# Layer 0's positional products: two bands of four offset rows side by side, in place of one block of eight

## The chip, the cores and the metric

The kernel runs on one core of one Trainium2 chip. The metric is the device time of that core for one execution, in microseconds. Before the change its median over three runs is 1242.21 us (1241.89 to 1242.93).

A core has several engines that run side by side, each through its own list of instructions in a fixed order: TensorE (PE, matrix products; PEld is its loading of weights), VectorE (DVE), ScalarE (ACT), GpSimd (POOL) and SyncE (SP), which here only issues transfers (DMAs). They wait for one another by semaphores. PSUM is the memory that TensorE writes its products to, in banks of 128 partitions by 512 fp32 numbers; SBUF is the working memory.

## The reference, cut to what matters

The input is four images of 16 x 16 positions and 1024 channels. Layer 0 is a lambda layer: queries q for four heads, keys k and values v, and two terms, one by content and one by position:

```python
q = bn(einsum('bhwc,cd->bhwd', x, Wq)); k = x @ Wk; v = bn(x @ Wv)   # x is group-normalised
q = q.reshape(b, heads, 256, m); k = softmax(k.reshape(b, 1, 256, m)); v = v.reshape(b, 1, 256, m)
Lc  = einsum('bukm,buvm->bkv', k, v)
Yc  = einsum('bhkn,bkv->bnhv', q, Lc)
rel = rel_pos_emb[rel_pos[..., 0], rel_pos[..., 1]]   # rel_pos = pos[m] - pos[n] + 15, in both directions
Lp  = einsum('nmku,buvm->bnkv', rel, v)
Yp  = einsum('bhkn,bnkv->bnhv', q, Lp)
x   = x + Yc + Yp
```

Layer 1 is causal attention with 16 heads and then a mixture of eight experts, each behind a layer norm. The change touches only the positional term of layer 0.

A position n is a row ni and a column nj of the 16 x 16 grid, likewise m. The table rel_pos_emb has 31 x 31 offsets with 256 numbers each; position n needs the entry (mi - ni + 15, mj - nj + 15) for every m.

## The kernel before, in words

**The order of the sums.** The kernel never forms Lc or Lp. It first makes one matrix of scores, s0[m, n, bh] = sum over the 256 key channels of (k[m] + rel[n, m]) times q[n, bh], for the 16 pairs bh of image and head, and then multiplies s0 with v (the products `py`, line 559).

**The positional scores (lines 446 to 482).** For one column nj, the 16 offsets mj - nj + 15 are 16 neighbouring columns of the table, and a whole row of offsets can serve every ni. So the loop takes the offset rows in blocks R of eight, in the order 1, 2, 0, 3. For each R and each of the 16 nj, GpSimd copies a window of the table (`emb`, two halves of 128 channels, eight offset rows by 16 columns) into one of four buffers (line 462). TensorE takes the window as its weights, 128 x 128 for each channel half, and streams past it the queries of all ni that need any of these rows: 16, 15, 8 and 7 rows ni for R = 1, 2, 0, 3, times the 16 bh (line 464). The result has 128 partitions, one for each offset row and mj. ScalarE and VectorE in turn copy two or four nj at a time out of PSUM into `two_T` (line 472).

In `two_T` a partition means an offset row; in s0 it means a row mi, and which one depends on ni. That shift is made by transfers: for each ni, one or two DMAs on SyncE's queue (line 479) move the right partitions of `two_T` to their partitions of s0, which holds mi in two halves of eight rows. There are 60 of them. Blocks 0 and 3 reuse the half of `two_T` that block 1 was copied out of.

**What stands around it.** Before it come the q and k products (lines 376 and 407); the k products already use the two column halves of TensorE side by side, each with 64 columns of weights. After it come the v products (`v_product`, line 493), seven of them with four pieces each, which read the normalised input `xn`. Then `x_at`, the raw input in eight tiles of 128 tokens, is loaded on SyncE's queue (line 537). It lies in the same buffer as `xn`, so its first load waits for the last v product.

Then comes a loop over the eight tiles (lines 547 to 577), first the four with positions ni >= 8 and then the four with ni < 8. `content(b, nt)` (line 422) adds the content scores to that half of s0; the products `py` multiply s0 with v; VectorE adds them to `x_at` (line 566) and a layer norm follows. The banks for `pT`, `py` and half of `pc` come from a tag "mm" with three banks (line 123):

```python
    def mm(name):
        return ps.tile([P, HALF], F32, tag="mm", name=name)
```

**What sets the order.** Inside `tc.manual_schedule(engines={SP, DVE})`, which begins after x_at's loads, SyncE and VectorE keep the order in which the loop is written. Elsewhere a planner sets each engine's order when the kernel is built; it may take a later instruction first where an earlier one isn't ready. In the profile, some products of line 496 stand ahead of those of line 464. SyncE's queue is one list: the table's load (line 241), the load of w_kv, the 60 copies of line 479, the eight loads of x_at, the load of w_v, and the transfers of the layer norms.

Of the kernel before, what the change touches and what calls it, by code (L numbers as in the profile page):

```python
# [32 lines left out]
F32 = mybir.dt.float32  # L33
# [6 lines left out]
P = 128  # L40
# [7 lines left out]
BH = B * HEADS0  # L48
SIDE = 16
REL = 2 * SIDE - 1  # L50
GROUP = 32
H = 16
D = C // H
# [2 lines left out]
HALF = 512  # L56
# [11 lines left out]
def kernel(  # L68
# [27 lines left out]
    nc = tc.nc  # L96

    def pool(stack, name, bufs=1, **kw):
        return stack.enter_context(tc.tile_pool(name=name, bufs=bufs, reuse_waits="tile", **kw))
# [10 lines left out]
    def big_tile(n, name, shape=(NC, TOK)):  # L110
        return big[n].tile([P, *shape], F32, tag="big", name=name)
# [11 lines left out]
    def mm(name):  # L123
        return ps.tile([P, HALF], F32, tag="mm", name=name)
# [85 lines left out]
    with ExitStack() as layer0:  # L210
# [9 lines left out]
        for i, a in enumerate((v_gamma, v_beta, v_mean, v_var)):  # L220
            nc.gpsimd.dma_start(vp[:, i, :], a)
        emb = l0.tile([P, 2, REL, REL], F32, tag="emb", name="emb")
        v_T = l0.tile([P, 2, TOK], F32, tag="v_T", name="v_T")

        q0 = l0.tile([P, 2, SIDE, SIDE, BH], F32, tag="q0", name="q0")

        with ExitStack() as projection:
# [3 lines left out]
            nc.vector.memset(average, 0.0)  # L231
            for g in range(P // GROUP):
                nc.vector.memset(average[ts(g, GROUP), ts(g, GROUP)], 1.0 / GROUP)
            first_root = small.tile([P, 1], F32, tag="first_root", name="first_root", bufs=1)
# [3 lines left out]
            q_scale, q_shift, mean_q, var_q = (q_rows[:, i, :] for i in range(4))  # L238
            for t, a in ((var_q, q_var), (q_scale, q_gamma), (mean_q, q_mean), (q_shift, q_beta)):
                nc.sync.dma_start(t, a.partition_broadcast(P))  # L240
            nc.sync.dma_start(emb.rearrange("p c i j -> p c (i j)"), embT)


            chunks = {}
# [72 lines left out]
            with tc.manual_schedule():  # L317
# [6 lines left out]
                for c in range(NC):  # L324
# [10 lines left out]
                    elif NC - 4 < c < NC - 1:  # L335
                        n = c - (NC - 3)
# [12 lines left out]
            parts = big_tile(0, "q_parts").rearrange("p a b -> p (a b)")  # L349
            b11, b12, b21, b22 = (w_q[l][:, 4 * j : 4 * j + 4, :] for j in range(2) for l in range(2))  # L350
            pairs = []
            for pair in range(2):
                a = [xn[:, 4 * j : 4 * j + 4, ts(4 + 2 * pair + i, P)] for i in range(2) for j in range(2)]
                homes = [parts[:, ts(8 * pair + i, HALF)] for i in range(8)]
# [47 lines left out]
            for t in range(NT):  # L402
                b, kc = divmod(t, 2)
                pk = (tr if t % 2 else mm)(f"pk{t}")
                for c in range(NC):
                    for kl in range(2):
# [4 lines left out]
                            start=(c == 0),  # L411
                            stop=(c == NC - 1),
# [28 lines left out]
        S2 = SIDE // 2  # L441
        s0 = big_tile(0, "s0", (2, SIDE, SIDE, BH))
        tpool = pool(layer0, "tpool", 2)
        two_T = big_tile(1, "two_T", (2, SIDE, SIDE, BH))

        for R, first, n_i, T in (
            (1, 0, 16, two_T[:, 0, :, :, :]),
            (2, 0, 15, two_T[:, 1, :15, :, :]),
            (0, 8, 8, two_T[:, 0, :8, :, :]),
            (3, 0, 7, two_T[:, 0, 8:15, :, :]),  # L450
        ):
            rows = min(S2, REL - S2 * R)
            parts = rows * SIDE
            group = 2 if n_i > S2 else 4
            for n0 in range(0, SIDE, group):
                pT = mm(f"pT{R}_{n0}")
                out_T = pT[:parts, : group * BH * n_i].rearrange("p (j i h) -> p j i h", j=group, h=BH)
                for g in range(group):
                    nj = n0 + g
                    at = SIDE - 1 - nj  # L460
                    window = tpool.tile([P, 2, rows, SIDE], F32, tag="window", name=f"window{R}_{nj}", bufs=4, padded_shape=[P, 2, S2, SIDE])
                    nc.gpsimd.tensor_copy(window, emb[:, :, S2 * R : S2 * R + rows, at : at + SIDE])
                    for kc in range(2):
                        nc.tensor.matmul(  # L464
                            out_T[:, g, :, :],
                            window[:, kc, :, :].rearrange("p i j -> p (i j)"),
                            q0[:, kc, first : first + n_i, nj, :],
                            start=(kc == 0),
                            stop=(kc == 1),
                        )  # L470
                evict = nc.scalar.copy if n0 // group % 2 == 0 else nc.vector.tensor_copy
                evict(T[:parts, :, n0 : n0 + group, :].rearrange("p i j h -> p j i h"), out_T)
            for i in range(n_i):
                ni = first + i
                start = S2 * R + ni - SIDE + 1
                for mh in range(2):
                    lo, hi = max(start, mh * S2), min(start + rows, mh * S2 + S2)
                    if lo < hi:
                        nc.sync.dma_start(
                            s0[(lo - mh * S2) * SIDE : (hi - mh * S2) * SIDE, mh, ni, :, :],  # L480
                            T[(lo - start) * SIDE : (hi - start) * SIDE, i, :, :],
                        )

# [63 lines left out]
        with tc.manual_schedule(engines={mybir.EngineType.SP, mybir.EngineType.DVE}):  # L547
            for i, (b, nt) in enumerate(tiles):
# [5 lines left out]
                for hp in range(2):  # L554
                    py = mm(f"py{t}_{hp}")
                    for hl in range(2):
                        bh = b * HEADS0 + 2 * hp + hl
                        for mh in range(2):
# [4 lines left out]
                                start=(mh == 0),  # L563
                                stop=(mh == 1),
# [16 lines left out]
    with ExitStack() as attention:  # L581
# [18 lines left out]
        T = [s_pool.tile([P, NC // 2, HALF], F32, tag=f"T{i}", name=f"T{i}", bufs=1) for i in range(3)]  # L600
# [275 lines left out]
    rows = dram.tile([TOK, C], F32, name="rows")  # L876
# [83 lines left out]
    with ExitStack() as gating:  # L960
# [306 lines left out]
        w, bias, step, T, T3, A, S = {0: w0}, {0: bias0[0]}, {}, {}, {}, {}, {}  # L1267
# [243 lines left out]
def _laid_out(inputs):  # L1511
    import numpy as np

    def get(name):
        return np.asarray(inputs[name])

    def columns(a):
        return a.reshape(-1, P).T
# [3 lines left out]

    emb = get("L0_conv_rel_pos_emb").reshape(REL * REL, 64, 2, 2).transpose(3, 1, 2, 0)
    return {
# [42 lines left out]
```

## Time and profile before

| what | value |
| --- | --- |
| median of 3 runs | 1242.21 us |
| the profiled execution's own time | 1242.44 us |
| its span | 1240.6 us |
| granted TensorE clock, mean | 0.999 |
| TensorE busy | 1224.4 us |
| VectorE, ScalarE, GpSimd busy | 740.2, 221.1, 390.8 us |
| positional products, line 464 | 148.47 to 188.68 us |
| copies into s0, line 479 | issued from 163.31 to 203.9 us |
| x_at's loads, line 537 | issued from 210.35 us |

The span is the time from the first to the last instruction of the core in the profile. A line of a view names the line of the code, the engine, the operation, the tile written and those read, the shapes, and a count. In the list of groups, the figures behind the bar are the busy time in us, the mean length of one in ns, and the idle time of the engine ahead of them. In the view in order of time, the first two figures are start and length in us, and a square bracket says how long the engine had been idle and for what it waited. In the list of waits, the figures are us in all, how often, and the longest.

### The profile page before, as it was taken

How to read it: one execution, taken by the hardware profiler on the slowest of the kernel's cores; microseconds unless marked ns; L12 is line 12 of the kernel's file. 1: busy time of each engine (PE TensorE's matmuls, PEld its weight loads, DVE VectorE, ACT ScalarE, POOL GpSimd, SP SyncE). 2: the span in 40 equal slices, each digit the busy share in tenths (PEclk: the TensorE clock that was granted, in tenths of full speed). 3: DMA queues.
4: the chain of work that ended last, by engine and by line, in shares of the span. 5: the costliest groups of instructions: out<-in, count | busy, mean ns of one | idle time of the engine just before them, and what ended most of it. 6: DMA issues, size and time to landing. Idle time of an engine off the chain costs nothing.

```text
span 1240.6 us, 12777 instructions
## 1 busy us (share of the span) xinstructions
PE 1224.4 (99%) x4540; PEld 639.8 (52%) x4540; DVE 740.2 (60%) x1322; ACT 221.1 (18%) x515; POOL 390.8 (31%) x471
## 2 busy tenths in 40 slices
PE   9999999999999999999999999999999999999998
PEld 5445894778884444444444444444344434434443
DVE  5796626677333666657554867766656656565642
ACT  3310111130001222223121431101111111111110
POOL 1041360340000222222230115445452735363521
PEclk9999999999999999999999999999999999999999
DMA  9002024842201535353393557383855575556432
GB/s 350 21 1 84 2 75 127 308 153 85 68 17 52 157 104 168 102 176 105 108 278 111 207 202 250 71 238 85 242 135 166 110 229 155 150 138 187 101 82 54
DMA packets 91495, 169.22 MB, mean 136 GB/s; under 512 B 9344, under 2 KB 46224, under 8 KB 91424
## 3 DMA queue, kind: packets, MB, share of 16 engines
q1 hardware_dynamic: 74064, 115.83, 27.9%
q0 software_dynamic: 15136, 47.78, 16.1%
q10 hardware_dynamic: 2224, 4.72, 1.1%
q8 instruction: 38, 0.62, 0.2%
q14 instruction: 33, 0.27, 0.1%
HBM read 115.59 MB, written 48.50 MB: 132 GB/s over the span
## 4 chain that ended last, share of the span: by engine, by line
PE 74%; DVE 3%; ACT 1%; issue 0%; DVEq 0%; ACTq 0%
PE p L1334 31%; PE pqk L616 16%; PE po L798 7%; PE pv L616 7%; PE left L1376 3%; PE sc L711 2%; PE pa L780 2%; PE rest L1390 2%; PE last_pe L1492 1%; PE dense_pe L918 1%; PE parts L1056 0%; ACT L132 0%; DVE row_T L177 0%; DVE xb L800 0%; DVE T L1277 0%
## 5 line engine op out<-in xcount | busy, mean ns | idle before, releaser
L903 POOL DMA_INDIRECT w_e_xg<-rows,gather x146 | 158.0, 1082 | 57.3 <-issue 40.8
L1334 PE MATMUL p<-w_e,A 128*128 128x512 f32 x368 | 163.2, 593 | 1.3 <-DVE slot L1169 1.3
L753 POOL TENSOR_TENSOR s_q<-s_q,total 128x128 f32<-128x128 f32 (+1 forms) x128 | 66.2, 547 | 300.3 <-DVE total L750 297.9
L798 PE MATMUL po<-w_p,y_T 128*128 128x512 f32 x256 | 118.5, 605 | 0.0
L1334 PEld LDWEIGHTS p<-w_e,A 128*128 128x128 f32 x368 | 69.6, 190 | 89.9 <-issue 89.9
L1334 PE MATMUL p<-T,S 128*128 128x512 f32 x256 | 112.7, 592 | 0.0
L926 POOL DMA_INDIRECT out_dram<-y,add x32 | 56.6, 1770 | 176.0 <-ACT y L1340 112.5
L1340 ACT ACTIVATE y<-y,slot 128x512 f32<-128x512 f32 x64 | 46.0, 722 | 330.6 <-DVE y L1348 165.2
L739 ACT ACTIVATE s_q<-s,top 128x256 f32<-128x256 f32 (+1 forms) x128 | 56.6, 444 | 186.1 <-issue 142.0
L616 PE MATMUL pqk<-ln,w_qk 128*128 128x512 f32 x192 | 85.6, 595 | 0.0
L1334 PEld LDWEIGHTS p<-T,S 128*128 128x128 f32 x256 | 48.6, 190 | 60.8 <-issue 60.5
L798 PEld LDWEIGHTS po<-w_p,y_T 128*128 128x128 f32 x256 | 45.9, 190 | 47.9 <-issue 46.9
L177 DVE STREAM_TRANSPOSE A<-w_e_xg 128x1024 f32<-128x1024 f32 x32 | 39.6, 1238 | 50.1 <-DMA w_e_xg<-rows,gather 50.1
L616 PE MATMUL pqk<-T,S_qk 128*128 128x512 f32 x128 | 58.5, 599 | 0.0
L616 PEld LDWEIGHTS pqk<-ln,w_qk 128*128 128x128 f32 x192 | 36.0, 190 | 43.3 <-issue 42.3
L1334 PE MATMUL p<-w_e,S 128*128 128x512 f32 x128 | 57.5, 592 | 0.0
L1334 PE MATMUL p<-T,A 128*128 128x512 f32 x128 | 57.5, 592 | 0.0
L616 PE MATMUL pv<-w_v,ln 128*128 128x256 f32 x192 | 44.2, 381 | 1.4 <-DVE ln L177 0.9
L295 PE MATMUL pq<-w_q,xn 128*128 128x512 f32 x96 | 44.5, 599 | 0.3 <-ACT xn L275 0.3
L1376 PE MATMUL left<-w_e,one 128*32 128x512 f32 x312 | 41.8, 593 | 0.0
L464 PE MATMUL pT<-q,window 128*128 128x256 f32 (+3 forms) x256 | 40.4, 320 | 0.0
L1334 PEld LDWEIGHTS p<-w_e,S 128*128 128x128 f32 x128 | 24.3, 190 | 30.6 <-issue 30.4
(317 smaller groups left out, 1871.8 us busy)
## 6 DMA issues: line engine op xcount, KB each, us to landing
w_e<-in_expert_w_dram SPq DMA_DIRECT2D x14, 2048.0 KB, 15.1
s_rows<-s_q SPq DMA_DIRECT2D x32, 384.0 KB, 2.7
s_rows<-s_rows SPq DMA_DIRECT2D x128, 96.0 KB, 2.2
w_qk<-in_W_attnT_dram SPq DMA_DIRECT2D x8, 1024.0 KB, 6.1
xn<-in_xT_dram SPq DMA_DIRECT2D x8, 512.0 KB, 7.5
w_q<-in_Wq_dram SPq DMA_DIRECT2D x16, 256.0 KB, 7.3
x_at<-in_x_dram SPq DMA_DIRECT2D x8, 512.0 KB, 4.8
w_v<-in_W_attnT_dram SPq DMA_DIRECT2D x2, 2048.0 KB, 14.5
```

Of the source, the lines that this page charges most:

```text
L177: nc.vector.transpose(row_T[:, :, :slots].rearrange("p c (g j) -> p g c j", j=32), row[:, : slots // 32, :].rearrange("p g (c i) -> p g c ...
L295: nc.tensor.matmul(pq, xn[:, c, ts(t, P)], w_q[kc][:, c, :], start=(c == 0), stop=(c == NC - 1))
L464: nc.tensor.matmul(out_T[:, g, :, :], window[:, kc, :, :].rearrange("p i j -> p (i j)"), q0[:, kc, first : first + n_i, nj, :], start=(kc ...
L616: nc.tensor.matmul(bank, stationary(c), moving(c), start=(c == 0), stop=(c == NC // 2 - 1))
L739: nc.scalar.activation(blocks(h, qt), s[:, h, cols].rearrange("p (b f i) -> p b f i", f=Q, i=32), AF.Exp, bias=top[:, qt, h : h + 1], accu ...
L753: nc.gpsimd.tensor_mul(blocks(h, qt), blocks(h, qt), total[:, qt, h : h + 1].unsqueeze(2).unsqueeze(3).to_broadcast([P, 1 + qt, Q, 32]),)
L798: nc.tensor.matmul(po, y_T[:, c, ts(t, P)], w_p[j][:, c, :], start=(c == 0), stop=(c == NC - 1))
L903: nc.gpsimd.indirect_dma_start(out=row[:, g, :], out_offset=None, in_=table[: (TOK - P) * Q, :] if e in SHORT else table, in_offset=bass.I ...
L926: nc.gpsimd.indirect_dma_start(out=out[: TOK - P, :] if e in SHORT else out, out_offset=bass.IndirectOffsetOnAxis(ap=add[:slots, e, k : k ...
L1334: nc.tensor.matmul(bank, a[:, c, :], b[:, c, :], start=(c == 0), stop=(c == NC // 2 - 1))
L1340: nc.scalar.mul(y[i][:, ts(j, HALF)], y[i][:, ts(j, HALF)], slot[:, e, 1, 2 * pair + i : 2 * pair + i + 1])
L1376: nc.tensor.matmul(bank[ts(i, 32), :], stationary, w[of][j][:, c, :], start=(c == 0), stop=(c == NC - 1))
```

## The change

The offset rows are taken in bands of four instead of blocks of eight. Two bands, one from below the middle and one from above it, are taken together: (3, 4), (2, 5), (1, 6), (0, 7). Each gives 64 columns of weights (48 for band 7, which has three rows), and the two use the two column halves of TensorE, so that they can stream different rows ni at the same time: 16, 12, 8 and 4 rows for the four pairs. The table is loaded in band order, by eight DMAs in place of one, so that a pair's rows lie side by side and one copy makes the window for both. In the last two pairs VectorE makes every second window. There are six window buffers in place of four.

The copies into s0 are listed as they become possible and issued in another order: after the first pair those with ni < 8, which frees the place that the third pair's results need, then those with ni >= 8; after every other pair those with ni >= 8; and at the end all that are left. They still stand ahead of x_at's loads in the program.

```diff
+BAND = 4
+BANDS = ((3, 4), (2, 5), (1, 6), (0, 7))
...
-            nc.sync.dma_start(emb.rearrange("p c i j -> p c (i j)"), embT)
+            at = 0
+            for band in (b for both in BANDS for b in both):
+                rows = min(BAND, REL - BAND * band)
+                nc.sync.dma_start(
+                    emb[:, :, at : at + rows, :].rearrange("p c i j -> p c (i j)"),
+                    embT[:, :, BAND * REL * band : (BAND * band + rows) * REL],
+                )
+                at += rows
...
-        for R, first, n_i, T in (
-            (1, 0, 16, two_T[:, 0, :, :, :]),
-            (2, 0, 15, two_T[:, 1, :15, :, :]),
-            (0, 8, 8, two_T[:, 0, :8, :, :]),
-            (3, 0, 7, two_T[:, 0, 8:15, :, :]),
-        ):
-            rows = min(S2, REL - S2 * R)
-            parts = rows * SIDE
-            group = 2 if n_i > S2 else 4
+        moves = []
+
+        def bands(k, half, band, n, first, T):
+            rows = min(BAND, REL - BAND * band)
+            for i in range(n):
+                ni = first + i
+                start = SIDE - 1 - ni
+                for mh in range(2):
+                    lo = max(BAND * band - start, mh * S2)
+                    hi = min(BAND * band + rows - start, mh * S2 + S2)
+                    if lo < hi:
+                        at = half * 64 + (lo + start - BAND * band) * SIDE
+                        to = s0[(lo - mh * S2) * SIDE : (hi - mh * S2) * SIDE, mh, ni, :, :]
+                        moves.append((k, ni, to, T[at : at + (hi - lo) * SIDE, i, :, :]))
+
+        def move(which):
+            for m in [m for m in moves if which(*m[:2])]:
+                nc.sync.dma_start(*m[2:])
+                moves.remove(m)
+
+        homes = (two_T[:, 0, :, :, :], two_T[:, 1, :12, :, :], two_T[:, 0, :8, :, :], two_T[:, 1, 12:, :, :])
+        for k, ((low, high), T) in enumerate(zip(BANDS, homes)):
+            n_i = BAND * (low + 1)
+            firsts = SIDE - n_i, 0
+            both = [min(BAND, REL - BAND * band) * SIDE for band in (low, high)]
+            parts = 64 + both[1]
+            group = HALF // (n_i * BH)
+            while SIDE % group:
+                group -= 1
             for n0 in range(0, SIDE, group):
...
-                    window = tpool.tile([P, 2, rows, SIDE], F32, tag="window", name=f"window{R}_{nj}", bufs=4, padded_shape=[P, 2, S2, SIDE])
-                    nc.gpsimd.tensor_copy(window, emb[:, :, S2 * R : S2 * R + rows, at : at + SIDE])
+                    rows = sum(both) // SIDE
+                    window = tpool.tile([P, 2, rows, SIDE], F32, tag="window", name=f"window{k}_{nj}", bufs=6, padded_shape=[P, 2, S2, SIDE])
+                    (nc.vector if k > 1 and nj % 2 else nc.gpsimd).tensor_copy(window, emb[:, :, S2 * k : S2 * k + rows, at : at + SIDE])
                     for kc in range(2):
-                        nc.tensor.matmul(
-                            out_T[:, g, :, :],
-                            window[:, kc, :, :].rearrange("p i j -> p (i j)"),
-                            q0[:, kc, first : first + n_i, nj, :],
-                            start=(kc == 0),
-                            stop=(kc == 1),
-                        )
+                        for half in range(2):
+                            nc.tensor.matmul(
+                                out_T[half * 64 : half * 64 + both[half], g, :, :],
+                                window[:, kc, BAND * half : BAND * half + both[half] // SIDE, :].rearrange("p i j -> p (i j)"),
+                                q0[:, kc, firsts[half] : firsts[half] + n_i, nj, :],
+                                start=(kc == 0),
+                                stop=(kc == 1),
+                            )
...
-            for i in range(n_i):
-                ni = first + i
-                start = S2 * R + ni - SIDE + 1
-                for mh in range(2):
-                    lo, hi = max(start, mh * S2), min(start + rows, mh * S2 + S2)
-                    if lo < hi:
-                        nc.sync.dma_start(
-                            s0[(lo - mh * S2) * SIDE : (hi - mh * S2) * SIDE, mh, ni, :, :],
-                            T[(lo - start) * SIDE : (hi - start) * SIDE, i, :, :],
-                        )
+            for half, band in enumerate((low, high)):
+                bands(k, half, band, n_i if half == 0 else REL - SIDE - BAND * (band - BANDS[0][1]), firsts[half], T)
+            if k == 0:
+                move(lambda k, ni: ni < S2)
+            move(lambda k, ni: ni >= S2)
+        move(lambda k, ni: True)
```

More of the change, by code (lines that the diff above doesn't have):

```diff
@@ L444 @@
         two_T = big_tile(1, "two_T", (2, SIDE, SIDE, BH))
-        for R, first, n_i, T in (
-            (1, 0, 16, two_T[:, 0, :, :, :]),
-            (2, 0, 15, two_T[:, 1, :15, :, :]),
-            (0, 8, 8, two_T[:, 0, :8, :, :]),
-            (3, 0, 7, two_T[:, 0, 8:15, :, :]),
-        ):
-            rows = min(S2, REL - S2 * R)
-            parts = rows * SIDE
-            group = 2 if n_i > S2 else 4
+        moves = []
[24 more added lines that the diff above has]
+                group -= 1
             for n0 in range(0, SIDE, group):
-                pT = mm(f"pT{R}_{n0}")
-                out_T = pT[:parts, : group * BH * n_i].rearrange("p (j i h) -> p j i h", j=group, h=BH)
+                pT = mm(f"pT{k}_{n0}")
+                out_T = pT[:, : group * BH * n_i].rearrange("p (j i h) -> p j i h", j=group, h=BH)
                 for g in range(group):
@@ L463 @@
                     for kc in range(2):
-                        nc.tensor.matmul(
-                            out_T[:, g, :, :],
-                            window[:, kc, :, :].rearrange("p i j -> p (i j)"),
-                            q0[:, kc, first : first + n_i, nj, :],
-                            start=(kc == 0),
-                            stop=(kc == 1),
-                        )
-                evict = nc.scalar.copy if n0 // group % 2 == 0 else nc.vector.tensor_copy
-                evict(T[:parts, :, n0 : n0 + group, :].rearrange("p i j h -> p j i h"), out_T)
@@ new lines @@
+                evict = nc.scalar.copy if n0 // group % 2 == 0 else nc.vector.tensor_copy
+                evict(T[:parts, :, n0 : n0 + group, :].rearrange("p i j h -> p j i h"), out_T[:parts])
+            for half, band in enumerate((low, high)):
[4 more added lines that the diff above has]
+        move(lambda k, ni: True)
```

## The prediction

> **What bounds the kernel now.** I read the page's engine totals first, then busy time by stage around the changed loop, then SyncE's own queue, then the two engines behind it in order of time.
>
> ```profile
> PE 1224.4 (99%) x4540; PEld 639.8 (52%) x4540; DVE 740.2 (60%) x1322; ACT 221.1 (18%) x515; POOL 390.8 (31%) x471
> ```
>
> TensorE is never free for long; a change pays only if it shortens TensorE's own work or leaves it fed. Groups kept apart by shape give what the positional products (L464) and their nearest column-split relatives (L407, L1128) cost:
>
> ```profile
> L407 PE MATMUL pk<-w_kv,xn 128*64 128x256 f32 x256 | 27.9, 380 | 0.0
> L464 PE MATMUL pT<-q,window 128*128 128x256 f32 x64 | 14.0, 379 | 0.0
> L464 PE MATMUL pT<-q,window 128*128 128x240 f32 x64 | 13.1, 366 | 0.0
> L464 PE MATMUL pT<-q,window 128*128 128x128 f32 x64 | 7.3, 275 | 0.0
> L464 PE MATMUL pT<-q,window 128*112 128x112 f32 x64 | 6.5, 262 | 0.0
> L1128 PE MATMUL lists<-entry,one 128*32 128x64 f32 x124 | 3.4, 225 | 0.0
> ```
>
> Two records stand for one fp32 product. L464 runs from 148.47 to 188.68 us, 40.2 us without a gap. L407 is the key: 128 pairs of half-array records in 27.9 us are 0.218 us a pair, what one full-array record of 256 columns costs (14.0 / 64 = 0.219). So two column halves do run side by side here.
>
> The queue that carries the results on is SyncE's:
>
> ```profile
> 163.31 40.60 SPq L479 DMA_DIRECT2D s<-two_T  x60
> 210.35 4.25 SPq L537 DMA_DIRECT2D x_at<-in_x_dram  x8
> ...
> SPq L537 <- PE pv L496: 6.3, 1, 6.3
> ```
>
> The 60 copies into s0 keep SyncE busy for the whole 40.6 us: it, not TensorE, sets their end (203.9). Single starts lie 0.6 to 0.7 us apart for 16 as for 128 partitions, 0.632 without three long steps that add 2.7 in all. Then SyncE waits 6.3 us for the last v product before it can issue x_at. That 6.3 us is all the slack on this queue. What stands behind x_at, in order of time:
>
> ```profile
> 217.02 3.69 PE L559 MATMUL py<-v_T,s 128*128 128x256 f32 x16
> 220.55 3.60 PE L428 MATMUL pc<-q,k_q 128*128 128x512 f32 x8
> 223.98 3.72 PE L559 MATMUL py<-v_T,s 128*128 128x256 f32 x16
> ...
> 218.97 0.69 DVE L566 TENSOR_TENSOR x_at<-x_at,py 128x512 f32<-128x512 f32 x1 [1.06 <-PE py L559]
> ...
> DMA to landing us min/median/max: 3.8/4.8/5.9
> ```
>
> The last line is x_at's. The first x_at lands about 210.35 + 3.8 = 214.2; VectorE's first add (L566) starts at 218.97 and waits for TensorE, not for x_at. The "mm" tag has three banks, taken in the order pc0, pc1, py0a, py0b, pc2, py1a: py1a (223.98) needs py0a's bank, free when that add ends (219.66). So x_at may come 4.8 us later before VectorE waits, and 4.3 us more before TensorE does.
>
> **What the Trainium skill says.** "TensorEngine Tiling (Array Packing)", Key Properties: tiles run weight loads and matmuls independently; L407 agrees. "TensorE: Matmul & The Clock Gate", the section "Wait — 56ns, not 53.3ns?": starts of small matmuls never come closer than about 25 ns; L1128, 3.43 us for 124, gives 27.7. Same page, "What's actually happening": an idle window of some 3.4 us halves the clock, and a busy window of that length restores it. The trace shows the cold end once: the first 28 warm-up products of 128 columns take 5.3 us, against 28 x 0.114 = 3.2 warm. It shows no re-throttling, because TensorE never idles that long. "DMA: Bandwidth & Descriptors", "Issuing engines are not separate DMA queues": the issue time on the sequencer is "usually small relative to the DMA itself". Here it isn't: 0.63 us each, back to back, against 2.1 us to landing.
>
> **The change, part by part.**
>
> *TensorE.* Pairs of half-array records, 64 per stage, with 256, 192, 128 and 64 columns in place of 256, 240, 128 and 112. By the rows above, a pair costs 0.219, 0.166 (between the rows for 240 and 128), 0.114, and 0.055 to 0.062 (two at L1128's pace, or the line carried on): 14.0 + 10.6 + 7.3 + 3.8 = 35.7 us against 14.0 + 13.1 + 7.3 + 6.5 = 40.9. That is 5.2 less; scaled to the 40.2 us on the clock 5.1, and I allow 0.4 for late windows: 4.7 us.
>
> *Windows.* Still 64 copies, 0.40 us each on GpSimd; 16 go to VectorE in the last two stages, six buffers in place of four. A last-stage window is used up in about 0.25 us; GpSimd at 0.40 and VectorE at some 0.35 (its 128x256 step on k_q, L420, takes that) together deliver one in about 0.2. VectorE's copies stand behind its evictions; stage 2's evictions reuse two_T[:, 0, :8] and wait for the first 19 copies into s0 (issued by 163.3 + 19 x 0.632 = 175.3, landed 177.4, where 174.9 would be wished). Cost 0 to 3 us of TensorE, hidden by the wait below; without that cover it would come out of the 4.7.
>
> *emb's load.* Eight issues for one at 24.6 us; nothing else is on SyncE until 104.3, the first window at 133.3. Nothing; uncovered, some 8 x 0.6 us. Evictions: 22 for 24, nothing.
>
> *Copies into s0.* Counting the pieces that lie in each half of the positions: 37 in stage 0 (19 with ni < 8, 18 with ni >= 8), then 14 + 8 + 4 with ni >= 8, and 25 held to the end: 88 for 60, same bytes. All 88 stand ahead of x_at on SyncE. Stage 0 costs what block 1 did, so the first is issued at 163.3 again. The end: 163.3 + 88 x 0.632 = 218.9, plus the long steps; 2.7 per 60 would be 4.0, none is the lower end; I take 3.4: 222.3. The ni >= 8 half (63 copies) has landed by about 208, in time for content's first add at 207.4.
>
> *What is late next.* v products finish 4.7 us earlier, at about 205.2, so x_at no longer waits for them but for SyncE: first issue 222.3 instead of 210.35, landing 3.8 later at 226.1. VectorE's add then ends at 226.8, and behind it in its written order stand the statistics and content's adds of the next tile. TensorE does pc0, pc1, py0 and pc2 and is at py1a by 223.98 - 4.7 = 219.3; it idles until 226.9. Against 223.98 that is +2.9: TensorE's gain is swallowed whole, and more. VectorE is then short of slack for two tiles (pc3's bank comes perhaps 0.2 late), and after that TensorE bounds again at 7 us a tile, so the delay stays to the end.
>
> *Restart.* TensorE has idled 7.6 us, so by the skill it restarts at half clock. Not seen in this trace: 0 if it doesn't, 3.4 if two windows pass; one window and the 5.3 - 3.2 above give about 2.0. I take 2.0.
>
> Sum: +2.9 + 2.0 = +4.9 us. The span goes from 1240.6 to 1245.5; the profiled execution took 1242.44, 1.8 outside its span and 0.2 over the median of 1242.21, so the median becomes 1247.1.
>
> **Rivals.**
>
> *Faster.* The copies issue quickly enough. For: some starts are 0.5 apart, the pieces are smaller (16 to 64 partitions), the long steps may not scale. Against: the step hardly depends on size. The decision point: x_at issued before 223.98 - 0.8 - 3.8 = 219.4, thus 0.637 per copy, everything included (the kernel before: 0.677), is break-even without a cold clock; at 214.7 (0.58) TensorE no longer idles and the whole 4.7 stays: 1237.5.
>
> *Late, but warm.* The issues end near 219 to 222 and the clock isn't throttled: +0.5 to +3, about 1244.
>
> *content waits for all 88 copies.* If the dependency on s0 isn't kept apart by ni, content's adds start at 222.3 + 2.1 = 224.4, py0 at 225.9 instead of 217.02: +8.9, plus the cold 2.0: 1253. Against: before, evictions of block 0 into two_T[:, 0, :8] run at 177.27 while copies out of its other rows are still being issued, so overlaps are judged by region.
>
> *No net effect.* Idle and gain happen to cancel: 1242.
>
> **How the numbers follow.** Late and cold 0.50 (own range 1245 to 1249.5), late but warm 0.18, faster 0.17 (1237.5 to 1240.5), content waits 0.10, no effect 0.05. A measurement of this kernel can tell about 0.2%, 2.5 us. Faster 0.17; same 0.05 and half of late-but-warm, 0.14; slower the rest, 0.69. The range 1239.0 to 1250.5 leaves out the better half of the faster case and nearly all of "content waits", some 0.17.
>
> **What would show it.** L464's stage about 35 us long; the SyncE burst 88 long and about 59 us; x_at issued near 222 with no wait for a v product; VectorE's first L566 add near 226, waiting for x_at's transfer; TensorE's one idle stretch of about 7 us just before, followed by some 4 us of matmuls at twice the step. I am wrong if x_at is issued before 219, if the planner places it ahead of the last 25 copies, or if TensorE stays fed past 220.

## The result and the profile after

| | before | after |
|---|---|---|
| median of the runs | 1242.21 us (1241.89 to 1242.93) | 1253.41 us (1249.82 to 1256.35, 5 runs) |
| profiled execution | 1242.44 us | 1253.85 us |
| its span, granted clock | 1240.6 us, 0.999 | 1252.0 us, 0.993 |

The changed kernel is slower: the ratio is 1.0086, with a 95% interval of 1.0065 to 1.0106. The forecast of 1247.1 us had the sign right, but the time lies above its range of 1239.0 to 1250.5. The profiled spans differ by 11.4 us; where those come from is the question.

The engine totals of the changed kernel:

```profile
PE 1225.3 (98%) x4796; PEld 633.7 (51%) x4796; DVE 744.2 (59%) x1337; ACT 220.2 (18%) x514; POOL 383.3 (31%) x455
```

TensorE is busy 0.9 us longer than before although the change shortens its work: in two stretches, shown below, it runs at half of its full rate ("half clock"), which stretches matmuls, and that counts as busy. The span grew by 11.4, so most of the loss is idle.

The groups of the positional products, by shape (busy time, mean ns of one record, idle ahead of them):

```profile
L495 PE MATMUL pT<-q,window 128*64 128x256 f32 x128 | 14.0, 380 | 0.0
L495 PE MATMUL pT<-q,window 128*64 128x192 f32 x128 | 10.6, 326 | 0.0
L495 PE MATMUL pT<-q,window 128*64 128x128 f32 x128 | 7.4, 273 | 0.7 <-ACT two_T L503 0.7
L495 PE MATMUL pT<-q,window 128*64 128x64 f32 x64 | 4.0, 223 | 0.0
L495 PE MATMUL pT<-q,window 128*48 128x64 f32 x64 | 3.9, 220 | 0.0
```

The stages took 14.0, 10.5, 7.4 and 4.2 us on the clock (in the last, records of 64 and 48 partitions overlap), 36.1 us for 40.2. The idle 0.7 in the third is the eviction waiting for the first copies out of two_T's rows. So the change does what it says: TensorE reaches content's first product at 205.92 us, 4.2 us earlier than before (210.15).

SyncE's queue in order of time (start, length, instruction, count):

```profile
163.22 58.74 SPq L472 DMA_DIRECT2D s<-two_T  x88
222.08 3.95 SPq L564 DMA_DIRECT2D x_at<-in_x_dram  x8
226.07 0.47 SPq L121 DMA_DIRECT2D w_v<-in_W_attnT_dram  x1
230.69 0.33 SPq L207 DMA_DIRECT2D ln_rows<-ln_rows  x1
244.45 1.85 SPq L174 DMA_DIRECT2D ln_quarters<-ln_rows  x4
```

The first three lines are what was forecast: 88 copies in a row, and x_at right behind them with no wait for a v product. x_at lands in 3.7/6.5/9.3 us (min, median, max; before 3.8/4.8/5.9). The last two are what the forecast did not look at: the first tile's layer norm goes out to DRAM (L207) and comes back in quarters (L174), and it stands behind x_at's 4 MB and the first w_v load's 2 MB. Its write takes 13.7 us to land: w_v lands at 243.1, 17.0 us after its issue, and the write 1.3 us later. TensorE behind it (each tile has sixteen `py` records):

```profile
226.59 5.31 PE L586 MATMUL py<-v_T,s 128*128 128x256 f32 x16 [6.66 <-DVE x_at L593]
...
235.17 3.71 PE L586 MATMUL py<-v_T,s 128*128 128x256 f32 x16
...
251.40 3.78 PE L437 MATMUL pc<-q,k_q 128*128 128x512 f32 x4 [3.85 <-DVE s L445]
254.97 4.71 PE L586 MATMUL py<-v_T,s 128*128 128x256 f32 x16
259.52 5.31 PE L437 MATMUL pc<-q,k_q 128*128 128x512 f32 x12
```

Beside the same products of the kernel before (tiles three and five, and the content products after):

```profile
230.97 3.71 PE L559 MATMUL py<-v_T,s 128*128 128x256 f32 x16
...
244.90 3.71 PE L559 MATMUL py<-v_T,s 128*128 128x256 f32 x16
248.44 5.31 PE L428 MATMUL pc<-q,k_q 128*128 128x512 f32 x12
```

There are two losses. At tile three the changed kernel is 235.17 - 230.97 = 4.20 us late, which is the forecast loss. At the next comparable place, 259.52 - 248.44 = 11.08: another 6.88 us, made of 3.85 us of waiting, four content records that take 3.78 instead of 1.88, and 4.71 instead of 3.72 for the `py` records after them (3.85 + 1.90 + 0.99 = 6.7). The rest to 11.4 comes by the end.

VectorE tells who waits for what. After, in order of time:

```profile
225.85 1.28 DVE L593 TENSOR_TENSOR x_at<-x_at,py 128x512 f32<-128x512 f32 x2 [12.17 <-DMA x_at<-in_x_dram]
...
249.53 1.25 DVE L179 STREAM_TRANSPOSE ln<-ln_quarters 128x1024 f32<-128x1024 f32 x1 [7.67 <-DMA ln_quarters<-ln_rows]
250.69 1.25 DVE L445 TENSOR_TENSOR s<-s,pc 128x512 f32<-128x512 f32 x2
```

Before, SyncE and then VectorE at the same steps:

```profile
230.48 2.57 SPq L172 DMA_DIRECT2D ln_quarters<-ln_rows  x4
```

```profile
237.78 1.25 DVE L177 STREAM_TRANSPOSE ln<-ln_quarters 128x1024 f32<-128x1024 f32 x1
```

Before, the turn of the first tile (L177) follows VectorE's other work without a wait. After, the quarters are issued 244.45 - 230.48 = 13.97 us later while TensorE is only 4.20 late, and the turn (L179) waits 7.67 us. In VectorE's written order content's adds stand right behind the turn, and they empty the banks that TensorE waits for.

The transfers in the same stretch. The columns are PE, PEld, DVE, ACT and POOL busy (instructions), TensorE's clock, the DMA engines' busy share and GB/s:

```profile
210.00:220.00 10.00, 9.93 (x31) 6.09 (x29) 1.62 (x3) 0.00 (x0) 0.00 (x0) 1.00 0.36 82
220.00:230.00 10.00, 3.41 (x9) 2.79 (x10) 3.78 (x10) 0.78 (x2) 0.00 (x0) 0.66 0.73 264
230.00:240.00 10.00, 10.00 (x36) 7.42 (x36) 6.72 (x14) 2.11 (x3) 5.85 (x4) 1.00 1.02 388
...
250.00:260.00 10.00, 8.60 (x22) 5.84 (x23) 8.40 (x16) 1.44 (x2) 2.90 (x2) 0.66 0.57 183
```

The clock falls to a mean of 0.66 in the two stretches in which TensorE starts again after its waits; over 251.3 to 255 us alone it is 0.50. The transfers are two thirds idle while SyncE still issues small copies, and full once x_at and w_v come. Their 6 MB (6.29 million bytes) would take about 16 us at 388 GB/s.

### The profile page after: what moved, and what is told of

Same layout as the page of the kernel before. It is cut to its first block, busy times and chain, and to the rows that moved or that the text cites. A ratio compares the mean times of both kernels' runs of the same rounds, so it can differ in the third digit from the quotient of the medians.

```text
span 1252.0 us, 13310 instructions
## 1 busy us (share of the span) xinstructions
PE 1225.3 (98%) x4796; PEld 633.7 (51%) x4796; DVE 744.2 (59%) x1337; ACT 220.2 (18%) x514; POOL 383.3 (31%) x455
## 4 chain that ended last, share of the span: by engine, by line
PE 74%; DVE 2%; ACT 1%; issue 0%; DVEq 0%; ACTq 0%
PE p L1361 31%; PE pqk L643 16%; PE pv L643 7%; PE po L825 7%; PE left L1403 3%; PE sc L738 2%; PE pa L807 2%; PE rest L1417 2%; PE last_pe L1519 1%; PE dense_pe L945 1%; PE parts L1083 0%; ACT L134 0%; DVE row_T L179 0%; DVE xb L827 0%; DVE T L1304 0%
## 5 line engine op out<-in xcount | busy, mean ns | idle before, releaser
L179 DVE STREAM_TRANSPOSE A<-w_e_xg 128x1024 f32<-128x1024 f32 x32 | 39.6, 1239 | 47.8 <-DMA w_e_xg<-rows,gather 47.8
L603 POOL TENSOR_TENSOR x_at<-x_at,ln_rows 128x1024 f32<-128x1024 f32 x8 | 19.4, 2427 | 78.5 <-ACT ln_rows L162 73.4
L643 PEld LDWEIGHTS pv<-w_v,ln 128*128 128x128 f32 x192 | 37.3, 196 | 6.4 <-ACT v L666 1.2
```

The lines of the kernel that those rows point to most:

```text
L179: nc.vector.transpose(row_T[:, :, :slots].rearrange("p c (g j) -> p g c j", j=32), row[:, : slots // 32, :].rearrange("p g (c i) -> p g c ...
L643: nc.tensor.matmul(bank, stationary(c), moving(c), start=(c == 0), stop=(c == NC // 2 - 1))
```

## The experiments

Each ratio is to the kernel before on the same chip. Its median there was 1243.57 us beside the 28 copies, x_at ahead, 25 copies on GpSimd and w_v behind the third tile; 1244.11 beside the 10 copies, the seven products and 14 copies on GpSimd; 1243.06 beside the two kernels with w_v in pieces; 1243.03 beside the last three. The question moves along: first whether the number of copies is the cause, then which of their followers hurts.

**28 copies more in the kernel before, and 10 more.** Nothing of the change but its count: copies already made are repeated, with the same data.

```diff
...
+                        nc.sync.dma_start(*copy)
+                        if R > 1:
+                            made.append((ni < S2, copy))
+        for _, copy in sorted(made, key=lambda m: m[0])[:28]:
+            nc.sync.dma_start(*copy)
```

> The kernel before, with its blocks of eight rows, and 28 of its 60 copies into s0 issued a second time at the end (same data to the same place): 88 issues as in the change, TensorE's work untouched. Theory (the number of issues on SyncE is the whole loss, and TensorE's saving is swallowed by the wait for x_at): x_at is issued near 222 and the time is that of the changed kernel, 1251 to 1255. Rival (something else in the bands costs the time): 1242 to 1247.

Measured 1255.3 us, ratio 1.0093 (1.0076 to 1.0110). SyncE, then TensorE:

```profile
220.71 4.49 SPq L543 DMA_DIRECT2D x_at<-in_x_dram  x8
```

```profile
225.84 3.93 PE L565 MATMUL py<-v_T,s 128*128 128x256 f32 x16 [1.36 <-DVE x_at L572]
...
251.46 3.78 PE L428 MATMUL pc<-q,k_q 128*128 128x512 f32 x4 [6.04 <-DVE s L436]
```

The count alone costs as much as the whole change. But the wait for x_at is small here, 1.36 us, since the old products end 4.2 later; the large wait is the one at 251, which the forecast had no term for. The repeats cost nothing by writing s0 once more: content's first add starts at 212.40, in the kernel before at 212.07.

With `[:10]` in place of `[:28]`:

> The kernel before, with 10 of its copies into s0 issued a second time at the end: 70 issues. Theory (SyncE has 6.3 us to spare ahead of x_at, 10 copies' worth): SyncE is through near 210.3, x_at is issued within 1 us of where it was, and the time is that of the kernel before within 0.1%. Rival (each further copy costs its issue time): a third of e4_before_plus28's loss, 4 us more.

Measured 1244.41 us, ratio 1.0005 (0.9998 to 1.0011), x_at at 210.67. Ten copies fit in the 6.3 us that SyncE spent waiting for the v products: that slack was read rightly.

**x_at ahead of the last 25 copies.**

```diff
-        move(lambda k, ni: True)
...
-            nc.sync.dma_start(xs[t], x[ts(t, P), :])
+            x_load = nc.sync.dma_start(xs[t], x[ts(t, P), :])
+        with tc.issue_after(x_load.ins):
+            move(lambda k, ni: True)
```

> The changed kernel, with x_at's eight loads placed ahead of the last 25 copies (ni < 8) on SyncE's queue. Theory (the late x_at is the first loss, the layer norm's transfer behind a 2 MB load the second): x_at is issued near 206 us, when the last v product frees its place, instead of 222; VectorE's first add into x_at starts near 214.8 and waits for TensorE; TensorE doesn't idle ahead of the second tile's py products, which start near 219.8 instead of 226.6. The first layer norm's transfer now stands behind the 25 copies (226.5), so the first turn may come up to 3 us late: 1238 to 1242 us. Rival (the loss lies in the narrow products or in content's wait for the copies): it stays at 1250 or above.

Measured 1250.19 us, ratio 1.0052 (1.0036 to 1.0069). The expectation failed. SyncE, then VectorE's first turn:

```profile
206.36 4.01 SPq L563 DMA_DIRECT2D x_at<-in_x_dram  x8
210.42 21.25 SPq L472 DMA_DIRECT2D s<-two_T  x25
231.78 0.82 SPq L207 DMA_DIRECT2D ln_rows<-ln_rows  x1
```

```profile
245.79 1.25 DVE L179 STREAM_TRANSPOSE ln<-ln_quarters 128x1024 f32<-128x1024 f32 x1 [12.19 <-DMA ln_quarters<-ln_rows]
```

The wait for x_at is gone, yet TensorE idles 6.7 us in the next place, behind a turn that waits 12.19. The 25 copies, now between x_at and the layer norm's write, take 0.85 us each. The w_v load has moved too: it is issued at 232.65, behind that write and ahead of its quarters, the first of which is issued at 235.81 and takes 7.3 us to land (before: 3.1). So a second limit lies behind x_at: the layer norm's round trip, which goes over the same queue and the same transfers.

**The last 25 copies on GpSimd's queue**, behind its last window (`on_pool`).

```diff
-        def move(which):
+        def move(which, queue=nc.sync):
...
-                nc.sync.dma_start(*m[2:])
+                queue.dma_start(*m[2:])
...
-        move(lambda k, ni: True)
+        with tc.issue_after(on_pool.ins):
+            move(lambda k, ni: True, nc.gpsimd)
```

> The changed kernel, with the last 25 copies issued by GpSimd, after its last window, instead of SyncE. Theory (SyncE's issue time is what delays x_at): SyncE is through with its 63 copies near 205, x_at is issued near 206, w_v near 210, and the first layer norm's transfer isn't behind anything new: 1238 us, the 4.2 us that TensorE saves. Rival (the number of small transfers, whoever issues them, is what costs): no better than 1250.

Measured 1239.93 us, ratio 0.9968 (0.9955 to 0.9980): faster than both kernels. GpSimd's queue, SyncE's, and VectorE's first turn:

```profile
188.86 8.59 POOL L472 DMA_DIRECT2D s<-two_T  x17 [0.17 <-issue]
```

```profile
208.05 4.05 SPq L567 DMA_DIRECT2D x_at<-in_x_dram  x8
...
228.44 2.53 SPq L174 DMA_DIRECT2D ln_quarters<-ln_rows  x4
```

```profile
234.92 1.25 DVE L179 STREAM_TRANSPOSE ln<-ln_quarters 128x1024 f32<-128x1024 f32 x1 [0.41 <-issue]
```

GpSimd is free and takes 0.5 us a copy. With x_at at 208.05 the turn waits for no transfer and TensorE keeps nearly all that the change saves: 1243.57 - 1239.93 = 3.6 of 4.2 us.

**The w_v load behind the third tile's layer norm**, all 88 copies on SyncE.

```diff
                 ln_done = layer_norm(ln_rows[:, i % 3, :], t, ln1, quarters, turns)
+                if i == 2:
+                    w_v0 = [w_tile("w_v0", W_attnT[:, 2 * C : 2 * C + HALF])]
...
```

> The changed kernel, with the first 2 MB load of w_v moved on SyncE's queue from behind x_at's loads to behind the third tile's layer-norm transfers. x_at stays late. Theory (the second loss comes from w_v's load in front of the first layer norm's transfer): that transfer lands some 5 us after its issue instead of 13.7, VectorE's first turn no longer waits 7.7 us, TensorE's second idle stretch (3.9 us at 247.5) and the half-speed products after it are gone, the first stay: 6.9 us less, 1246.5. Rival (x_at's own 4 MB, which come at the same late time, hold the transfer up): no change, 1253.

Measured 1251.31 us, ratio 1.0063 (1.0047 to 1.0080). Missed again, in a telling way. SyncE, then TensorE:

```profile
230.95 0.33 SPq L207 DMA_DIRECT2D ln_rows<-ln_rows  x1
237.41 2.40 SPq L174 DMA_DIRECT2D ln_quarters<-ln_rows  x4
...
251.73 0.43 SPq L121 DMA_DIRECT2D w_v<-in_W_attnT_dram  x1
252.26 0.52 SPq L207 DMA_DIRECT2D ln_rows<-ln_rows  x1
263.42 1.90 SPq L174 DMA_DIRECT2D ln_quarters<-ln_rows  x4
```

```profile
226.85 5.80 PE L586 MATMUL py<-v_T,s 128*128 128x256 f32 x16 [6.74 <-DVE x_at L593]
...
269.82 3.61 PE L586 MATMUL py<-v_T,s 128*128 128x256 f32 x14 [2.29 <-DVE s L445]
```

The quarters follow the first layer norm's write by 6.5 us in place of 13.8, and the wait at 247.5 is gone. But the moved load did the same to the fourth tile's trip, 11.2 us, and TensorE waits there.

**The same, with seven products into an unused bank where TensorE idles.**

```diff
+                if i == 1:
+                    warm = ps.tile([P, 2, HALF], F32, tag="sc", name="warm_x", bufs=1)
+                    with tc.issue_after(latest.ins):
+                        for _ in range(7):
+                            nc.tensor.matmul(warm[:, 0, :], ident, v_T[:, 0, :HALF], start=True, stop=True)
...
```

> The kernel of e3_wv_later (the change, with w_v's load moved behind the third tile's layer norm), and seven products of 128x512 into a bank that nobody reads, placed on TensorE between the third tile's content products and the second tile's py products, where it idles 6.7 us. They add work and take none from the result. Theory (TensorE restarts at half clock because it has idled): the second tile's py products take 3.7 us instead of 5.8, the next content products start 1.6 to 2.1 us earlier than in e3_wv_later, measured from the first add into x_at, and the granted clock stays at 1.0; the time is up to 2 us below e3_wv_later, less if the layer norm's transfers set the pace again. Rival (those products are slow for another reason, such as VectorE's use of the banks): they take 5.8 us again.

Measured 1253.7 us (1251.9 to 1256.26), ratio 1.0076 (1.0060 to 1.0093). TensorE in the profiled execution, the slowest of the four:

```profile
228.06 3.93 PE L592 MATMUL py<-v_T,s 128*128 128x256 f32 x16 [1.21 <-DVE x_at L599]
...
272.49 5.26 PE L592 MATMUL py<-v_T,s 128*128 128x256 f32 x14 [3.75 <-DVE s L445]
```

Kept busy, TensorE does the sixteen records after the wait in 3.93 us instead of 5.80: their length was the clock. The Trainium skill, "TensorE: Matmul & The Clock Gate", section "What's actually happening", says that an idle window, which it puts at about 3.4 us, halves the clock until a busy one has passed. The waits of 6.66 and 6.74 us agree; shorter waits that also halved it stand in the last section. But the kernel gained nothing. What TensorE no longer lost at the first place it waited for later: the first turn waits 3.72 us here and none in the kernel without the seven products. Here the layer norms, not TensorE, set the pace.

**14 of the last 25 copies on GpSimd, 11 left on SyncE**, so that x_at comes at 214, where the forecast had put the point from which all of the gain is kept.

```diff
+        with tc.issue_after(on_pool.ins):
+            move(lambda k, ni: k > 1 or ni > 5, nc.gpsimd)
         move(lambda k, ni: True)
```

> The changed kernel, with 14 of the last 25 copies issued by GpSimd and 11 left on SyncE: 74 copies ahead of x_at, which is then issued near 212.7. By the prediction's decision point (x_at issued before 214.7 keeps TensorE fed) the whole saving stays: the time of e2_last25_pool, 0.3% below the kernel before. Rival (the layer norm's transfers, behind x_at's and w_v's 6 MB, are the tighter bound): the first turn comes some 3 us late, TensorE idles in the third or fourth tile, and 1 to 4 us of the saving are gone.

Measured 1244.07 us (1241.53 to 1248.14), ratio 1.0002 (0.9994 to 1.0010). TensorE in the profiled execution, which took 1248.14 and so shows the upper end of the spread:

```profile
243.36 3.78 PE L437 MATMUL pc<-q,k_q 128*128 128x512 f32 x4 [3.67 <-DVE s L445]
```

The second tile's products do not wait, as the forecast's decision point has it; in the median the gain is lost all the same (the fastest execution keeps 2.6 us of it). In this execution it is lost at the turn, which waits 7.48 us. The layer norm's round trip is the tighter of the two limits.

**Is it w_v, or x_at's lateness itself?** Two kernels cut the first w_v load into eight pieces of 256 KB and issue them behind the layer norms of the first five tiles:

```diff
...
+                for c in {0: (0,), 1: (1,), 2: (2, 3), 3: (4, 5), 4: (6, 7)}.get(i, ()):
+                    nc.sync.dma_start(w_v0[:, c, :], W_attnT[ts(c, P), 2 * C : 2 * C + HALF])
...
```

With all copies on SyncE:

> The changed kernel (all 88 copies on SyncE, x_at issued at about 222), with the first w_v load cut into eight pieces of 256 KB that are issued behind the layer norms of the first five tiles (1, 1, 2, 2, 2 pieces), so that no 2 MB load stands ahead of the first layer norm's transfers. Theory A (the second loss is the layer norm's round trip queued behind x_at and w_v): x_at stays at 222, the second tile's products still wait some 6.7 us and run at half clock, but the first quarters are issued some 15 to 17 us after x_at instead of 22.4, the turn waits under 3 us and the TensorE idle of 3.85 us at 247.5 goes; only the first loss of about 4.2 us stays, so the ratio to the kernel before is 1.003 to 1.005. Theory B (the second loss is x_at's own lateness in VectorE's order, whatever w_v does, or the spread pieces delay the later layer norms as the moved w_v did): the ratio stays between 1.006 and 1.009.

Measured 1252.87 us, ratio 1.0079 (1.0062 to 1.0095). TensorE:

```profile
249.56 3.71 PE L586 MATMUL py<-v_T,s 128*128 128x256 f32 x16
...
270.09 5.26 PE L586 MATMUL py<-v_T,s 128*128 128x256 f32 x14 [2.85 <-DVE s L445]
```

At the fifth tile the kernel is 249.56 - 244.90 = 4.66 us late, in place of 10.07: the second loss is gone there, as Theory A says. It comes back in the tail. With the pieces among them the layer norms' writes take 5.6 us to land instead of 3.5 (medians), the last turns wait 2.6 to 3.1 us each, and TensorE idles before the last tile. In time, the second half of Theory B is right.

With 14 copies on GpSimd:

> The changed kernel with 14 of the last 25 copies on GpSimd (x_at issued at about 214) and the first w_v load in eight pieces behind the layer norms of the first five tiles. Theory A (w_v ahead of the layer norm's transfers made the 3.7 us of idle that the same split showed with w_v in one piece): the turn hardly waits, TensorE doesn't idle at 243, and the earlier positional products are kept to the end: ratio 0.996 to 0.998. Theory B (x_at at 214 is too late by itself, or the pieces cost the later layer norms what they save the first): ratio 0.999 to 1.003.

Measured 1244.37 us, ratio 1.0014 (1.0005 to 1.0023): no help either. TensorE's wait of 3.67 us, which was seen in the slowest execution of the kernel with w_v in one piece, is 0.72 here, and 1.78 us at 260.75 with a half clock takes its place. A load moved later among the layer norms costs them what it saves.

**The w_v load earlier instead.** GpSimd issues it as soon as the v products have freed its buffer, while the transfers are mostly idle.

```diff
         nc.gpsimd.dma_start(bp, b_proj.partition_broadcast(P))
+        w_v0 = w_tile("w_v0", W_attnT[:, 2 * C : 2 * C + HALF], queue=nc.gpsimd)
...
```

With all copies on SyncE:

> The changed kernel (all 88 copies on SyncE, x_at issued at about 222), with the first w_v load issued by GpSimd as soon as the v products have freed its buffer, some 16 us ahead of x_at, when the transfers are two thirds idle. Theory A (the second loss is the 2 MB of w_v between x_at and the layer norms' transfers, wherever among them they go): the second tile's products still wait some 6.7 us and run at half clock, +4.2 us, but the layer norms' trips take 2.6 to 4 us each, no later TensorE idle follows, and the ratio to the kernel before is 1.003 to 1.0045. Theory B (a layer norm chain that begins 11 us late costs TensorE more than the first idle by itself, with w_v or without): 1.006 to 1.009, with an idle of 2 us or more between 240 and 275.

Measured 1249.76 us, ratio 1.0056 (1.0039 to 1.0073). TensorE:

```profile
229.85 6.50 PE L587 MATMUL py<-v_T,s 128*128 128x256 f32 x16 [9.62 <-DVE x_at L594]
...
239.62 3.71 PE L587 MATMUL py<-v_T,s 128*128 128x256 f32 x16
...
253.56 3.71 PE L587 MATMUL py<-v_T,s 128*128 128x256 f32 x16
```

Tile three is 239.62 - 230.97 = 8.65 us late and tile five 253.56 - 244.90 = 8.66. Nothing is added between them: no turn waits, and the layer norms' writes land in 2.6 us (median; the first takes 5.8). That is the mechanism of Theory A. TensorE's larger delay also gives the turn more time, so the plainer sign is the time from x_at's issue to that of the quarters: 14.5 us instead of 22.4. The ratio lies above Theory A's range because the first loss grew: w_v's 2 MB lengthened the landing of some of the last 25 copies on SyncE from 2.0 us to as much as 7.5. In the program each copy waits for the one eight places ahead (one starts at 213.56, when that one has landed at 213.55). Three such waits take 2.7 us, and x_at was issued at 225.24 instead of 222.08; the idle and the half clock grew with it.

With 14 copies on GpSimd, the same edit:

> 14 of the last 25 copies on GpSimd (x_at at about 214) and the first w_v load on GpSimd ahead of x_at. Theory A: x_at at 214 is early enough once w_v isn't behind it; TensorE's idle of 3.67 us at 243 goes, the 4.2 us of the shorter positional products are kept: ratio 0.996 to 0.998. Theory B: x_at's own 4 MB hold the first layer norm: an idle of 1 us or more stays between 230 and 265 and the ratio is 0.999 to 1.002.

Measured 1239.12 us, ratio 0.9972 (0.9961 to 0.9983). TensorE:

```profile
238.62 3.70 PE L437 MATMUL pc<-q,k_q 128*128 128x512 f32 x8 [1.02 <-DVE s L445]
```

It is Theory A's ratio, though the wait of Theory B is there in part: TensorE idles 1.02 us at 238.62 in place of 3.67 at 243.36. The quarters follow the first layer norm's write by 6.6 us; without this edit they followed by 14.1. With x_at at 214.86, later than without this edit (214.03), the kernel is faster than before by 0.28%, where it had been equal. So w_v's place decides, at the same x_at.

**Both loads on GpSimd, all copies on SyncE.** The edit of the last two, and x_at's loop with `nc.gpsimd` in place of `nc.sync`.

> The changed kernel with x_at's eight loads and the first w_v load issued by GpSimd, which has nothing to do between its last window (183) and 230; all 88 copies stay on SyncE. Theory A (the copies cost nothing by themselves, only by standing ahead of the loads): x_at is issued at about 205 to 206, TensorE doesn't idle between 205 and 260, ratio 0.996 to 0.9975. Theory B (the copies and the loads share the transfers, or the first layer norm's write, issued on SyncE behind the copies at 222 or later, is late by itself): the loads take longer to land, the turn waits, and the ratio is 0.999 to 1.004.

Measured 1243.23 us, ratio 1.0007 (1.0000 to 1.0014). SyncE, then TensorE:

```profile
194.71 32.71 SPq L472 DMA_DIRECT2D s<-two_T  x43
228.14 0.37 SPq L207 DMA_DIRECT2D ln_rows<-ln_rows  x1
```

```profile
240.57 5.40 PE L437 MATMUL pc<-q,k_q 128*128 128x512 f32 x8 [3.43 <-DVE s L445]
```

Theory B holds. x_at is issued at 206.37 and nobody waits for it. But the 26 copies issued from 205.5 on, which share the transfers with its 4 MB and w_v's 2, land in 7.0 us (median) instead of 2.0 and go out 0.86 us apart; the layer norm's first write stands behind them until 228.14, where the kernel with 25 copies on GpSimd had it at 221.87. The turn waits 5.5 us. The Trainium skill, "DMA: Bandwidth & Descriptors", section "Issuing engines are not separate DMA queues", says that transfers interleave on the same engines whoever issues them; here that is the 2.0 that became 7.0.

## Why the prediction was wrong

*TensorE's gain*: 4.7 forecast, 4.2 measured. The groups were right (14.0, 10.6, 7.3 and 3.8 forecast, 14.0, 10.6 and 7.4 measured, 4.2 us for the last stage's stretch). Instead of the 0.4 allowed for late windows, 0.7 was lost to the evictions into two_T, which the forecast had named and taken to be hidden.

*The copies and x_at*: right. First copy at 163.3 forecast, 163.22 measured; x_at issued at 222.3, measured 222.08; VectorE's add at 226.1, measured 225.85; TensorE's restart at 226.9, measured 226.59. "content waits for all 88 copies" did not happen: its first add started at 207.91.

*The restart*: half clock, as forecast; 1.6 us in the second tile's products (5.31 for 3.72) where 2.0 stood.

*Sum of these*: +4.9 forecast, +4.20 at tile three. Up to there every step held.

*The step that failed*: "VectorE is then short of slack for two tiles (pc3's bank comes perhaps 0.2 late), and after that TensorE bounds again at 7 us a tile, so the delay stays to the end." It does not stay: it grows to 10.07 at tile five. The forecast followed x_at to its first reader and stopped. Behind x_at on SyncE and on the transfers stand w_v's 2 MB and the layer norm's trip to DRAM and back, and the turn that needs it stands ahead of content's adds in VectorE's order. The trace of before showed it: the four quarters are issued from 230.48 on, 20.1 us after x_at, the last at 232.6, and land some 3.1 us after their issue (median), at 235.7; the turn runs at 237.78. That is a slack of 2.1 us. Moving x_at by the forecast's own 12 us brings the quarters to 247.7, while VectorE, 4.2 us late like TensorE, comes to the turn at 242.0: an estimated wait of 5.7 us. Measured, VectorE came at 241.86 and waited 7.67, the trip from x_at to the quarters having grown from 20.1 to 22.4 us. The forecast had this wait nowhere.

*The decision point*: "at 214.7 (0.58) TensorE no longer idles and the whole 4.7 stays". It was worked out from the first reader alone. With w_v behind x_at, 214.03 gives no gain and 208.05 gives 3.6 of the 4.2 us; with w_v ahead, 214.86 gives 3.9.

*Rivals*: "Faster" fell with its condition, since x_at was issued at 222.08 and not before 219.4. "Late, but warm" and "No net effect" were wrong; both had the first loss only. The 1253 of "content waits" fits the measured time by chance, for another reason.

Shown by the runs: the extra issues on SyncE cause the loss; the half clock is real; the second loss is the layer norm's round trip behind x_at and w_v. It goes when w_v goes ahead, and moves along when w_v moves along. Left open: the last 0.3 us of the 11.4; how a kernel with all 88 copies on SyncE could keep the gain, since none of those tried did; and whether w_v ahead would add anything to 25 copies on GpSimd, which was not tried.

## What to carry to other kernels

When a queue of small DMAs grows, follow not only the first load behind it, but every load and store behind that one, to the last reader, and compare each reader's slack with how much later its data comes; the one with the least slack decides. A large load that nobody needs soon belongs ahead of a round trip that somebody does, and not among several (behind the last such trip was not tried here). Before moving issues to another queue, look at what shares the transfers as well: splitting the small copies over two queues before the loads start turned a loss of 0.9% into a gain of 0.3%.

## What the runs showed of the hardware

- A copy's step on SyncE's queue depends on what else is on the transfers: 58.74 / 88 = 0.67 us alone, 0.86 with x_at and w_v under way, 21.25 / 25 = 0.85 right behind x_at. In this program that comes from waiting for the DMA eight places ahead: right behind x_at, seven copies wait 5.4 us in all for x_at's loads. On GpSimd's queue it was 8.59 / 17 = 0.51.
- The first layer norm's write, issued 4.6 us behind a 2 MB load, took 13.7 us to land; with w_v out of the way behind the same x_at it took 6.5. The later writes of the kernel before took 2.6.
- A half clock followed waits of 6.66, 3.85 and 3.67 us, and also those of 2.85 and 1.78 (5.26 and 5.22 us for fourteen `py` records that take 3.61 after a wait of 2.29); waits of 1.36, 1.62 and 2.29 left the clock as it was. So the length of the wait alone did not decide it, and a wait well under the 3.4 us named above could halve the clock.
- Some kernels in which TensorE waits spread more: 1249.82 to 1256.35 for the changed kernel and 1241.53 to 1248.14 for the one with 14 copies on GpSimd, where the kernel before kept within 1242.45 to 1245.85 in 39 executions on the latter's chip. Others did not: the one with w_v ahead and all copies on SyncE kept within 1249.40 to 1250.41 (four executions).
